# A planner that counts less overlap between instructions, and products of zeros at the start: graph network with attention, one core

## The chip, the core and the metric

The kernel runs on one of the eight cores of a Trainium2 chip. A core has five engines that run beside each other, each with its own queue of instructions in a fixed order: TensorE (PE, matrix products), VectorE (DVE), ScalarE (ACT), GpSimd (POOL) and SyncE (SP, which here only issues DMAs). They wait for each other by semaphores. Products land in PSUM, which has eight banks; everything else works from SBUF. The metric is the device time of one execution in microseconds (us). Unless marked ns, times here are in us.

## What is computed

For each of 128 graphs (128 nodes, 256 features) and an adjacency `adj` of 0 and 1, two layers are applied. Cut to what matters:

```python
def gru_cell(inp, h):                      # w_ih, w_hh: (768, 256)
    gi = inp @ w_ih.T + b_ih
    gh = h @ w_hh.T + b_hh
    r = sigmoid(gi_r + gh_r); z = sigmoid(gi_z + gh_z)
    n = tanh(gi_n + r * gh_n)
    return (1.0 - z) * n + z * h

h = maximum(layernorm(x), 0)               # layer 0
for i in range(3):
    m = einsum('bnd,de->bne', h, weight[i])
    aggr = einsum('bst,bsd->btd', A, m)    # A = (adj != 0)
    h = gru_cell(aggr, h)
x = x + h

h = maximum(layernorm(x), 0)               # layer 1
Wh = h @ W
s = Wh.sum(-1)
e = leaky_relu(s[:, :, None] + s[:, None, :], 0.2)
e = where(adj == 0, -inf, e)
x = x + softmax(e, -1) @ Wh
```

## The kernel before

**Tiling and stages.** The graphs go in 32 groups of four. A group has three stages, one for each step of the recurrence, and then its attention. The first two stages (`gru`) work with features on the partitions: their products are the fp32 matmuls of L708, 128x256. The third (`gru_rows`) works with nodes on the partitions: its products are those of L722, 128x384, called "in rows" here. Stages of different groups follow each other by a fixed list (`turns`): in the steady part, layer 0 of group g, layer 1 of group g-1, layer 2 of group g-2. That makes 96 stages, 32 of them in rows.

**A stage's products.** Each large product is split in blocks so that seven products do the work of eight (sums and differences of the blocks are `hs`, from GpSimd, and `gs`, from VectorE). The seven go into six PSUM banks, x_rz, x_n, q_rz, q_n, y_rz and y_n, in the order written in `products`: x (product 1), q (product 5 or 7), y (product 6), y again (7 or 5), x (2), y (3 or 4), q (4 or 3). The bank y holds a running sum that is read off in between: after product 6 ScalarE copies y_rz to `t2_rz` and y_n to `t2_n`, and only then may the next product be added to y; after that product it copies them to `t3_rz` and `t3_n`, to which VectorE adds q (L764). These copies are all in the helper `put` (L754, or L758 and L760 with a bias). In the profile, whose names leave numbers out, t2_rz and t3_rz both read t_rz. So between "y_n, product 6" and "y_rz, the next product" TensorE depends on one ScalarE copy.

**Other work of TensorE.** Sums over edges in bf16 parts (L634, 24 products for a group and step), the attention's weighted sums (L663) and its rows product (L1099), and transposes (L544). It uses two further banks, `misc`.

**The planner.** Nothing of the order is written out by hand except the order of a stage's products among themselves. `op(engine, ns, fn, reads, writes, ...)` records a piece of work with an estimated duration; `Plan.run` then plays a list scheduler: at each step it finds for each engine the earliest time at which any of its ready pieces can start, takes among the pieces that can start then the one with the lowest rank (a latest start time, worked back from due times), and writes it to that engine's queue. The recurrence's products are a chain in fixed order (`bound`); the other pieces of TensorE go in where the next of the chain can't start yet, or where their rank is lower. A piece ends at `done = t + ns`, and its engine is free for the next at `done - OVER[engine]`: OVER is how far the next instruction overlaps the end of this one, in ns. `wait` and `LAG` give the time from a piece's end to its users. `port` serialises GpSimd with those VectorE pieces that share SBUF access with it (`two=True`).

**The start.** `zeros` is a bf16 tile; two products of it (L326) write 0 to the banks y_rz and y_n, which the first real products overwrite. Then `weights()` loads and transposes the weights. SyncE's first DMAs are: the first message weight (tile e), the two halves of w_ih (tile rz), the second message weight, the first rows of x, adj, w_hh, more rows. `turned` (L363) transposes w_ih half by half through PSUM, VectorE and ScalarE copy the results out (L371), and products (L463) compose them with the transposed message weight (L452) into the weight of the edge terms. w_hh is transposed in the same way, and `block_sums` (L382 to L390) makes the sums of blocks that the stages need.

Of the kernel before, what the change touches and what calls it, by code (L numbers as in the profile page):

```python
# [41 lines left out]
class Plan:  # L42
# [5 lines left out]


    LAG = {"PE": 163, "ACT": 0, "DVE": 0, "POOL": 0, "SP": 3600}  # L50
    OVER = {"PE": 0, "ACT": 103, "DVE": 84, "POOL": 42, "SP": 0}
    FLIP, HANDOFF = 56, 120
    SIGNAL = {"PE": 53, "ACT": 36, "DVE": 36, "POOL": 78, "SP": 28}

    def __init__(self, tags):
# [4 lines left out]
    def buf(self, tag):  # L60
        n, kind = self.tags[tag]
        if kind == "free" or kind == "turn":
            b = Buf(tag, tag, None)
            if kind == "turn":
                self.waiting.setdefault(tag, []).append((self.phase, len(self.waiting.get(tag, ())), b))
            return b
        key = (tag, self.group % SETS if kind == "set" else 0)
        uses = self.last.setdefault(key, [])
        b = Buf(tag, key, uses[-n] if len(uses) >= n else None)
        b.slot = (key[1], len(uses) % n)  # L70
        uses.append(b)
        return b

    def op(self, eng, ns, fn, reads=(), writes=(), room=(), due=None, mark=None,
           turn=None, two=False, lag=None, thin=False):

        i, deps = len(self.nodes), set()  # L80
        for b in room:
            if b.prev is not None:
                deps.update(a[0] for a in b.prev.accesses)
        for is_write, group in ((False, reads), (True, writes)):
            for item in group:
                b, lo, hi = item if isinstance(item, tuple) else (item, 0, 1 << 30)
                for j, w, l, h in b.accesses:
                    if (w or is_write) and l < hi and lo < h:
                        deps.add(j)
                if is_write and b.prev is not None:  # L90
                    deps.update(a[0] for a in b.prev.accesses)
        for is_write, group in ((False, reads), (True, writes)):
            for item in group:
                b, lo, hi = item if isinstance(item, tuple) else (item, 0, 1 << 30)
                b.accesses.append((i, is_write, lo, hi))
        deps.discard(i)
        bufs = {id(x[0] if isinstance(x, tuple) else x): (x[0] if isinstance(x, tuple) else x)
                for x in list(reads) + list(writes) + list(room)}
        free = [b for b in bufs.values() if self.tags[b.tag][1] in ("free", "turn")]
        for b in free:  # L100
            b.users.append(i)
            b.left += 1
        self.nodes.append([eng, ns, fn, deps, free, self.due if due is None else due,
                           two or eng == "POOL", self.LAG[eng] if lag is None else lag, thin])
        if due is not None:
            self.chain.append(i)
        if mark is not None:
            self.marks[mark] = i
        if turn is not None:
            self.turns.append((i, turn))  # L110

    def wait(self, i, u):

        a, b = self.nodes[i], self.nodes[u][0]
        return 0 if a[0] == b == "PE" else a[7] + self.SIGNAL[b]

    def run(self):
# [11 lines left out]
        for tag, w in waiting.items():  # L129
            n = self.tags[tag][0]  # L130
# [40 lines left out]
        order, end = [], 0.0  # L171
        while len(order) < len(nodes):
            best = None
            for e, pool in ready.items():
                if not pool:
                    continue
                starts = []
                for i in pool:
                    if i in bound and i != chain[-1]:
                        continue  # L180
                    t = max(clock[e] + (self.FLIP if thin and e == "PE" and not nodes[i][8] else 0), at[i])
                    for b in nodes[i][4]:
                        if b.slot is None:
                            t = max(t, min(slots[b.tag]))
                            if b.tag in waiting and waiting[b.tag][-1] is not b:
                                t = float("inf")
                    starts.append((max(t, port) if nodes[i][6] else t, t, i))
                first = min((t for t, _, _ in starts), default=float("inf"))
                if first == float("inf"):
                    continue  # L190
                asked, i = min(((r, i) for t, r, i in starts if t <= first), key=lambda x: (rank[x[1]], x[1]))
                if best is None or (first, asked) < best[:2]:
                    best = (first, asked, e, i)
            t, _, e, i = best
            ready[e].remove(i)
            if i in bound:
                chain.pop()
            n = nodes[i]
            done = t + n[1]
            clock[e] = done - self.OVER[e]  # L200
            if n[6]:
                port = done - self.HANDOFF
            if e == "PE":
                thin = n[8]
            end = max(end, done)
            for b in n[4]:
                if b.slot is None:
                    if b.tag in waiting:
                        waiting[b.tag].pop()
                    b.slot = (0, min(range(len(slots[b.tag])), key=lambda k: slots[b.tag][k]))  # L210
                    slots[b.tag][b.slot[1]] = float("inf")
                b.left -= 1
                b.done = max(getattr(b, "done", 0.0), done + n[7] + 36)
                if not b.left:
                    slots[b.tag][b.slot[1]] = b.done
            for u in users[i]:
                missing[u] -= 1
                at[u] = max(at[u], done + self.wait(i, u))
                if not missing[u]:
                    ready[nodes[u][0]].append(u)  # L220
            order.append(i)
# [5 lines left out]
def kernel(  # L227
# [84 lines left out]
    op, buf = plan.op, plan.buf  # L312
# [9 lines left out]

    zeros = const.tile([P, GN], BF16, name="zeros")
    nc.vector.memset(zeros, 0.0)
    for kind in ("y_rz", "y_n"):
        nc.tensor.matmul(phys[kind, 0, 0].rearrange("p q n -> p (q n)"), zeros[:, :P], zeros, start=True,  # L326
                         stop=True, skip_group_check=True)


    W = {t: buf(t) for t in ("s_hh", "s_x0", "s_x1", "s_x2", "bias_i", "bias_h", "bias_s", "bias_n", "seed_x",  # L330
# [3 lines left out]
    def bank(early=True):  # L334
        spare.append(spare.pop(0))
        return buf(spare[-1] if early else "misc")
# [14 lines left out]
    def nat(b):  # L351
        return plain(b)[:, :3 * KD * D].rearrange("p (c e) -> p c e", e=D)

    def turned(src, dst, evict, order=range(6)):


        for a in range(2):
            for k in range(KD):
                ps = bank()

                def turn(k=k, a=a, ps=ps):
                    for c in range(3):
                        nc.tensor.transpose(flat(ps)[:, c * P:(c + 1) * P],  # L363
                                            nat(src)[:, order[3 * a + c], k * P:(k + 1) * P],
                                            ident)
                op("PE", 330, turn, [(src, a, a + 1)], [ps])
                to_sbuf(evict[k % len(evict)], 3 * P, ps, dst[k], 3 * P * a)

    def to_sbuf(eng, cols, ps, dst, at):
        copy = nc.scalar.copy if eng == "ACT" else nc.vector.tensor_copy  # L370
        op(eng, 150 + cols, lambda: copy(plain(dst)[:, at:at + cols], flat(ps)[:, :cols]),  # L371
           [ps], [(dst, at, at + cols)])
# [20 lines left out]
    def weights():  # L393
        plan.due, plan.phase = 10 ** 9, -1
        w_hh_nat, w_ih_nat = buf("rz"), buf("rz")
# [13 lines left out]
        for a in range(2):  # L409
            part = slice(3 * a, 3 * a + 3)  # L410
            op("SP", 384 * KB, lambda part=part: nc.sync.dma_start(
                nat(w_ih_nat)[:, part], w_ih.rearrange("(c p) e -> p c e", p=P)[:, part]),
               [], [(w_ih_nat, a, a + 1)], lag=3300)
        plan.due = 10 ** 9
        load(w_hh_nat, nat, w_hh.rearrange("(c p) e -> p c e", p=P), 768)
        plan.due = -10 ** 8
# [14 lines left out]
        op("DVE", 250, n_bias, [W["bias_h"]], [W["bias_n"]])  # L431

        w_hhT, w_ihT = [buf("u"), buf("u")], [buf("x1"), buf("x1")]
        turned(w_ih_nat, w_ihT, ("DVE", "ACT"))

# [4 lines left out]
        for layer in range(L):  # L442
            if layer == 1:
                turned(w_hh_nat, w_hhT, ("DVE", "ACT"), (4, 5, 0, 1, 2, 3))
                block_sums(w_hhT, W["s_hh"], "POOL", 1000)
# [31 lines left out]
        for t, i, b in ((tmp[0], 0, b_ih), (tmp[1], 0, b_hh), (tmp[2], 0, b_hh), (tmp[2], 1, b_ih)):  # L477
            n = t is tmp[2]
# [55 lines left out]
    def flat(b):  # L534
        return ap(b).rearrange("p q n -> p (q n)")
# [679 lines left out]
```

## Time and profile before

| | us |
|---|---|
| median of 3 runs | 2112.8 |
| lowest and highest of them | 2112.46, 2113.26 |
| the profiled execution | 2112.71 |
| its span, first to last instruction | 2110.9 |

| engine | busy, us | instructions |
|---|---|---|
| TensorE, products | 2084.3 | 10624 |
| VectorE | 1680.2 | 3626 |
| ScalarE | 1594.6 | 2977 |
| GpSimd | 921.5 | 881 |

How to read it: a line of a group or a timeline has the source line, the engine, the operation and the tiles as out<-in; in a timeline the first number is the start from the span's beginning and the second the time from the start of the first to the end of the last of a merged row, and what stands in brackets is idle time of the engine before it and what ended it. Matmuls are pipelined and their ends are modelled: each is shown longer than the time to the next one's start. So the distance between starts tells TensorE's pace, and the sum of busy time does not. An fp32 product written once in the program is shown as two records. A step of 0.216 from start to start is the undisturbed pace of a 128x256 fp32 record, 0.323 that of 128x384.

### The profile page before, as it was taken

The numbers are of one execution on the slowest core, as the hardware profiler recorded it, in microseconds if no ns is written. First come the engines' busy times: TensorE is split into PE (matmuls) and PEld (weight loads), VectorE is DVE, ScalarE is ACT, GpSimd is POOL, SyncE is SP. The second block draws the span as 40 slices with busy tenths as digits, with TensorE's granted clock in tenths as the row PEclk, the third lists the DMA queues.
The fourth block names the chain that finished last, engine by engine and source line by source line (L and its number), as shares of the span: only waits on it lengthen the run. The fifth ranks groups of instructions, "written<-read, shape, count | busy, mean of one in ns | idle before, by whom it ended". The sixth has DMA issues, their size and how long they took to land.

```text
span 2110.9 us, 30632 instructions
## 1 busy us (share of the span) xinstructions
PE 2084.3 (99%) x10624; PEld 1658.4 (79%) x10624; DVE 1680.2 (80%) x3626; ACT 1594.6 (76%) x2977; POOL 921.5 (44%) x881
## 2 busy tenths in 40 slices
PE   9999999999999999999999999999999999999998
PEld 7887887777877778877778777788777888788776
DVE  6678888788877887878878778887787778778777
ACT  5577877777777777777777777777778877867676
POOL 5445554334444444443355434444443444345230
PEclk9999999999999999999999999999999999999999
DMA  4322222332233223232223332232322323123321
GB/s 120 70 59 48 56 57 65 71 60 55 68 68 80 55 54 72 68 73 70 55 61 63 73 74 57 55 75 63 78 60 55 70 64 78 36 55 66 77 74 36
DMA packets 365147, 137.01 MB, mean 65 GB/s; under 512 B 296384, under 2 KB 364736, under 8 KB 364992
## 3 DMA queue, kind: packets, MB, share of 16 engines
q1 hardware_dynamic: 364992, 135.05, 29.1%
q8 instruction: 84, 1.38, 0.3%
q14 instruction: 71, 0.58, 0.1%
HBM read 45.36 MB, written 16.78 MB: 29 GB/s over the span
## 4 chain that ended last, share of the span: by engine, by line
PE 79%; ACT 10%; DVE 7%; issue 2%; DMA 0%; POOL 0%; SPq 0%; DVEq 0%; ACTq 0%; POOLq 0%
PE y_rz L708 14%; PE x_rz L708 10%; PE q_rz L708 8%; PE y_n L708 7%; PE y_rz L722 5%; PE misc L1099 5%; PE y_n L722 5%; PE misc L634 5%; PE x_n L708 4%; PE q_n L708 4%; PE q_rz L722 3%; PE x_n L722 3%; PE x_rz L722 3%; PE q_n L722 3%; ACT h L530 2%
## 5 line engine op out<-in xcount | busy, mean ns | idle before, releaser
L677 POOL TENSOR_TENSOR hs<-hT 128x512 f32<-128x512 f32 x96 | 129.5, 1350 | 304.5 <-PE y_n L722 238.9
L591 POOL TENSOR_TENSOR r<-rows 128x512 f32<-128x512 f32 x126 | 143.0, 1154 | 225.3 <-ACT rows L574 160.9
L764 DVE TENSOR_TENSOR t_rz<-t_rz,q_rz 128x512 f32<-128x512 f32 x192 | 130.8, 681 | 132.5 <-ACT t_rz L754 123.4
L754 ACT COPY t_rz<-y_rz 128x512 f32<-128x512 f32 x192 | 112.2, 584 | 146.4 <-PE y_rz L708 136.1
L708 PE MATMUL y_rz<-hs,s_hh 128*128 128x256 f32 x768 | 200.0, 383 | 1.0 <-ACT t_rz L754 0.9
L708 PE MATMUL y_rz<-gs,s_x 128*128 128x256 f32 x768 | 197.1, 379 | 0.0
L708 PEld LDWEIGHTS y_rz<-hs,s_hh 128*128 128x128 f32 x768 | 142.8, 190 | 27.1 <-ACT t_rz L754 9.2
L708 PEld LDWEIGHTS y_rz<-gs,s_x 128*128 128x128 f32 x768 | 145.9, 190 | 19.8
L594 POOL TENSOR_TENSOR p<-r 128x512 bf16<-128x512 f32 x126 | 156.9, 1264 | 0.0
L681 POOL TENSOR_TENSOR hs<-hT,hs 128x256 f32<-128x256 f32 x96 | 75.3, 785 | 177.1 <-PE q_n L722 160.7
L834 ACT ACTIVATE u<-u,bias_i 128x512 f32<-128x512 f32 x128 | 92.8, 725 | 74.0 <-DVE u L825 73.8
L764 DVE TENSOR_TENSOR t_n<-t_n,q_n 128x512 f32<-128x512 f32 x192 | 130.3, 678 | 19.9 <-ACT t_n L754 17.8
L898 POOL TENSOR_TENSOR x<-x,u 128x512 f32<-128x512 f32 x60 | 77.6, 1294 | 147.9 <-ACT u L878 62.8
L708 PE MATMUL x_rz<-hT,s_hh 128*128 128x256 f32 x512 | 131.4, 379 | 0.0
L708 PE MATMUL x_rz<-aT,s_x 128*128 128x256 f32 x512 | 131.4, 379 | 0.0
L840 DVE SCALAR_TENSOR_TENSOR d<-rz,d 128x512 f32<-128x512 f32 x128 | 117.6, 920 | 0.9
L637 ACT COPY aT<-misc 128x512 f32<-128x512 f32 x190 | 102.8, 581 | 18.1 <-PE misc L634 17.9
L616 POOL TENSOR_TENSOR pl<-d,pl 128x512 bf16<-128x512 f32 x64 | 75.7, 1183 | 89.9 <-ACT pl L614 89.8
L708 PE MATMUL y_n<-gs,s_x 128*128 128x256 f32 x384 | 114.3, 379 | 0.0
L708 PE MATMUL y_n<-hs,s_hh 128*128 128x256 f32 x384 | 114.3, 379 | 0.0
L837 DVE TENSOR_TENSOR d<-hT,u 128x512 f32<-128x512 f32 x128 | 107.3, 839 | 8.5 <-ACT u L834 6.3
L611 POOL TENSOR_TENSOR d<-hT,pl 128x512 f32<-128x512 f32 x64 | 85.6, 1339 | 63.7 <-ACT pl L609 59.0
(286 smaller groups left out, 6297.9 us busy)
## 6 DMA issues: line engine op xcount, KB each, us to landing
rows<-in_x_dram SPq DMA_DIRECT2D x32, 512.0 KB, 4.2
x<-in_x_dram SPq DMA_DIRECT2D x32, 512.0 KB, 3.9
out_dram<-x SPq DMA_DIRECT2D x31, 512.0 KB, 2.9
at<-in_adj_dram SPq DMA_DIRECT2D x32, 256.0 KB, 3.2
plT<-pl SPq DMA_TRANSPOSE x186, 3.3
peT<-pe SPq DMA_TRANSPOSE x60, 3.1
e<-in_L_gnn_weight_dram SPq DMA_DIRECT2D x3, 256.0 KB, 3.7
rz<-in_L_gnn_w_ih_dram SPq DMA_DIRECT2D x2, 384.0 KB, 4.3
```

Of the source, the lines that this page charges most:

```text
L591: op("POOL", 1042, lambda part=part: nc.gpsimd.tensor_tensor(ap(r1)[:, part], ap(rows)[:, part], top(rows)[:, part], OP.subtract), [(rows, ...
L594: op("POOL", 1042, lambda part=part: nc.gpsimd.tensor_tensor(ap(p3)[:, part], ap(r1)[:, part], top(r1)[:, part], OP.subtract), [(r1, n, n ...
L634: nc.tensor.matmul(flat(ps)[:, b * N:(b + 1) * N], part(i, b, k), ap(a)[:, b, :], start=(i == 0), stop=(i == 2))
L637: op("ACT", 590, lambda k=k, ps=ps: nc.scalar.copy(ap(dst)[:, k, :], flat(ps)), [ps], [(dst, 2 * k, 2 * k + 2)])
L677: op(eng, cost, lambda: sub(ap(w)[:, 0:2, :], blocks()[:, 1::2, :], blocks()[:, 0:2, :], OP.subtract), [t], [(w, 0, 2)], two=True)
L708: nc.tensor.matmul(ap(bank)[:, half, :], ap(w)[:, i - 1, gate, :], source(i, t, sums), start=(first and c == 0 and m == 0), stop=False, sk ...
L722: op("PE", 645, lambda c=c, w=w, t=t, sums=sums: nc.tensor.matmul(flat(bank)[:, c * P:(c + 3) * P], source(i, t, sums)[:, m * N:(m + 1) * ...
L754: op("ACT", 590, lambda: nc.scalar.copy(ap(t), ap(y)), [y], [t], mark=mark)
L764: op("DVE", 690, lambda: nc.vector.tensor_tensor(ap(t), ap(t), ap(q), OP.add), [q], [t])
L837: op("DVE", 690, lambda j=j, d=d, cols=cols: nc.vector.tensor_tensor(ap(d), ap(hT)[:, j, :], ap(u)[:, cols], OP.subtract), [(hT, lo, hi), ...
L840: op("DVE", 690, lambda d=d, cols=cols: nc.vector.scalar_tensor_tensor(ap(d), ap(rz)[:, 1, cols], 1.0, ap(d), op0=OP.add, op1=OP.mult), [( ...
L1099: nc.tensor.matmul(ap(ps)[:, b, :], ap(uT)[:, k, (m + b) * N:(m + b + 1) * N], ap(w1)[:, k, :], start=(k == 0), stop=(k == KD - 1))
```

## The change

Three things are changed.

The overlap that the planner subtracts falls from 103 to 50 ns for ScalarE, from 84 to 40 for VectorE, and from 42 to -100 for GpSimd (its next instruction is now planned 100 ns after the end of the one before). The old numbers stay in a table, `TRUE`, that nothing reads. A piece of TensorE that the planner starts before 7200 ns is planned with twice its duration. And the second half of w_ih is planned to land 700 ns later. None of these changes an instruction by itself; they change the times by which `run` orders the queues.

Five products of zeros instead of two stand at the program's beginning, and `turned`, when it transposes w_ih, records three more (into y_n) between the two halves, to be run once the first half has landed.

Lines after L360 or so are 11 further on in the new kernel (L754 is L765, L722 is L733, L708 is L719).

```diff
-    OVER = {"PE": 0, "ACT": 103, "DVE": 84, "POOL": 42, "SP": 0}
-    FLIP, HANDOFF = 56, 120
+    OVER = {"PE": 0, "ACT": 50, "DVE": 40, "POOL": -100, "SP": 0}
+    TRUE = {"PE": 0, "ACT": 103, "DVE": 84, "POOL": 42, "SP": 0}
+    FLIP, HANDOFF, COLD = 56, 120, 7200
...
+    def ns(self, i, t):
+        return self.nodes[i][1] * (2 if self.nodes[i][0] == "PE" and t < self.COLD else 1)
...
-            done = t + n[1]
+            done = t + self.ns(i, t)
             clock[e] = done - self.OVER[e]
...
-    for kind in ("y_rz", "y_n"):
+
+    def nought(kind):
         nc.tensor.matmul(phys[kind, 0, 0].rearrange("p q n -> p (q n)"), zeros[:, :P], zeros, start=True,
                          stop=True, skip_group_check=True)
+
+    for kind in ("y_rz", "y_n", "y_rz", "y_n", "y_rz"):
+        nought(kind)
...
-    def turned(src, dst, evict, order=range(6)):
+    def turned(src, dst, evict, order=range(6), fill=0):
         for a in range(2):
+            if a == 1 and fill:
+                op("PE", 216 * fill, lambda: [nought("y_n") for _ in range(fill)], [(src, 0, 1)], [])
             for k in range(KD):
...
-               [], [(w_ih_nat, a, a + 1)], lag=3300)
+               [], [(w_ih_nat, a, a + 1)], lag=3300 + 700 * a)
...
-        turned(w_ih_nat, w_ihT, ("DVE", "ACT"))
+        turned(w_ih_nat, w_ihT, ("DVE", "ACT"), fill=3)
```

## The prediction

> **What bounds the kernel now.** I read the page first, then who TensorE waits for, then one stage's timelines, then the first 20 us.
>
> ```profile
> PE 2084.3 (99%) x10624; PEld 1658.4 (79%) x10624; DVE 1680.2 (80%) x3626; ACT 1594.6 (76%) x2977; POOL 921.5 (44%) x881
> ...
> engine line waited for: us in total, times, longest us
> PE y_rz L722 <- ACT t_rz L754: 14.1, 19, 1.3
> ```
>
> TensorE has work from end to end; no other engine is over 80%. So time can come only from TensorE's own stops, and most of what is printed is one wait, 19 times: the second edge term's product into y_rz, in the stage that is computed in rows (L722), waits for ScalarE's copy t_rz<-y_rz (L754). One of the 19, TensorE first, then ScalarE:
>
> ```profile
> 581.32 0.81 PE L722 MATMUL y_n<-s_hh,hs 128*128 128x384 f32 x2
> 581.97 0.81 PE L722 MATMUL y_n<-s_x,gs 128*128 128x384 f32 x2
> 583.45 0.91 PE L722 MATMUL y_rz<-s_hh,hs 128*128 128x384 f32 x2 [0.68 <-ACT t_rz L754]
> 584.20 0.81 PE L722 MATMUL y_rz<-s_x,gs 128*128 128x384 f32 x2
> 584.85 1.89 PE L1099 MATMUL misc<-w,uT 128*128 128x256 f32 x8
> ...
> 578.74 0.72 ACT L834 ACTIVATE u<-u,bias_i 128x512 f32<-128x512 f32 x1 [1.40 <-DVE u L825]
> 579.36 0.57 ACT L668 COPY uT<-misc 128x512 f32<-128x512 f32 x1
> 579.83 2.08 ACT L530 ACTIVATE h<-x,nm,rs 128x256 f32<-128x256 f32 x4
> 581.87 1.04 ACT L570 COPY pl<-hT 128x1024 uint16<-128x1024 uint16 x1
> 582.82 0.58 ACT L754 COPY t_rz<-y_rz 128x512 f32<-128x512 f32 x1
> ```
>
> Groups of two such products start 0.65 apart, so the third was due at 582.62. It came at 583.45 (0.83 late) and took 0.75 instead of 0.65 before the next: 0.93 lost, 0.25 more than the printed 0.68. Over the 19: 14.1 + 19 x 0.25 = 18.9; I use 18.5, since some of the added pace is rounding. ScalarE had been busy since 578.74, with an L570 directly ahead of the copy. And the eight L1099 products, which wait for nothing here, stand behind the stop, not in it.
>
> The start:
>
> ```profile
> 3.55 0.66 PE L452 MATMUL misc<-ident,e 128*128 128x128 f32 x2 [1.27 <-DMA e<-in_L_gnn_weight_dram]
> 5.33 0.85 PE L363 MATMUL x_rz<-ident,rz 128*128 128x128 f32 x3
> 7.19 0.87 PE L363 MATMUL misc<-ident,rz 128*128 128x128 f32 x3 [1.01 <-DMA rz<-in_L_gnn_w_ih_dram]
> 11.06 2.53 PE L463 MATMUL misc<-x,uT 128*128 128x512 f32 x4
> 14.29 1.88 PE L463 MATMUL misc<-x,uT 128*128 128x512 f32 x4
> ```
>
> The four L463 products at 11.06 took 2.36 to the next start (13.42); the same four at 14.29 took 1.71 (to 16.00). TensorE ran at half pace until about 12.4, with holes before 3.55 and 7.19.
>
> **What the Trainium skill says.** "TensorE: Matmul & The Clock Gate", Part 1: the array starts at half clock and gets full clock after about 3.4 us of sustained activity, in a free-running window. The trace agrees: after the hole at 7.19, 5.2 us of unbroken work at half pace. That products of zeros count as activity no run here shows. "ScalarE: Activation LUTs", in its section "What ACT_TABLE_LOAD costs", has back-to-back activations overlap by about 93 ns; the trace has 0.10 (592 ns each on average for L530, four in 2.08: (4 x 0.592 - 2.08) / 3). So the overlap counted before (103) is true and the new 50 is pessimistic. "SBUF — State Buffer", section "SBUF: two separate sides": VectorE and GpSimd lock each other out of a shared port; the trace has VectorE's L677 at 1.57 beside GpSimd's L591 and at 0.69 elsewhere. GpSimd's planned 1158 for L611 and L616 is 1339 and 1183 in the page, so counting -100 of overlap there is nearer the truth.
>
> **The change, part by part.** The numbers of overlap alter no instruction, only the order that the planner writes. TensorE's products of the recurrence keep their order; what is moved is the unbound work between them (L634, L663, L1099) and the queues of the other engines. I compared the orders of the two programs, by the old line numbers.
>
> *The 18.5 us.* Each of 96 stages has the place y_rz, y_n, then y_rz again behind the copy. Before, 2 of the 32 rows stages and 28 of the 64 others have unbound products in that place; after, 8 and 40. Before, 23 rows stages have them one step too late, behind the stalled y_rz, as above; after, 1. This is what a planner that takes ScalarE to be later must do: it sees the copy late and puts the products ahead. Where it leaves the place empty, it has found the copy in time by a slower ScalarE than the real one. In the steady part the old order repeats every group and the new one every five, so there are five rows stages. With the vector release of u at the same place (578.74) and 0.62, 0.47, 0.51 and 0.95 for L834, L668, one L530 and L570:
> - u, two L668, copy: 580.3.
> - u, two L668, two L570, copy: 582.2, some 0.2 late, but L1099 products (eight in the trace's count, 8 x 0.216 = 1.73) stand in the place.
> - u, four L530, a second u, copy: at least 582.0, just in time if the second u isn't late.
> - L570, L668, L570, L668, copy, from 577.2 on: 580.0.
> - two u, two L668, L614 (0.51), copy: 581.4 if the first u comes at 578.74.
> The copy must start by 582.0. So four of five are free, and one is covered. I keep 2.0 of the 18.5 for the third kind and the irregular groups: -16.5; bounds -18.5 and -10 (the third and fifth kind still lose 0.93, some 9 stages).
>
> *The small lag.* In stages that aren't in rows an empty place costs 0.08 (the group at 561.25 takes 0.94 instead of 0.86). Twelve more are filled: -0.8 (0.94 rounded down for added late copies).
>
> *TensorE's switches* from bf16 to fp32 go from 99 to 100, each 0.05 (the x_n at 574.32: 0.86 for 0.81): +0.05.
>
> *Five products of zeros instead of two.* At half pace 0.43 each (1.65 minus 1.25 is 0.40): five from 1.25 end at 3.4, and the first weights land at 3.42. They are covered; uncovered, +0.1. They and three more in the hole from 5.97 to 7.19 (1.28 at half pace, 0.65 at full) are there for the clock. If they count, full clock comes between 4.7 and 8.1 by the page's 3.4 us. From 7.19 the four L463 groups then run to about 11 instead of 16; but the new order puts a transpose of w_hh third, and w_hh landed at 12.55. So the gain isn't the 2.6 us that half of 7.19 to 12.4 gives, it is bound by that landing: 12.55, plus 0.33, 0.86, 1.0 and 1.7 of work, plus the transposes and the first products, puts the first q_rz<-hs (before at 26.13) at about 21.8, with four L463 (1.7) still to be done: 2.6 ahead, of which later waits for VectorE and GpSimd take some. I take -2.0; bounds -3.3 and +0.5 (no warmth, and the fill in the way).
>
> *The end.* The order of the last two groups changes in detail, after the last stages ScalarE and VectorE feed TensorE one graph at a time. No row prices it: 0, between -2 and +2.
>
> Sum: -16.5 - 0.8 + 0.05 - 2.0 + 0 = -19.2. The profiled execution is 2112.7, its span 2110.9, so 1.8 lies around it; the median is 2112.8. 2112.8 - 19.2 = 2093.6, taken as 2094.
>
> **The rivals.** A change under 0.2% (4.2 us) can't be told from none here.
> - *The stops move* (15%). Five kinds of groups have fifteen stages, each with a copy that a 1.0 us conversion can hold up. For it: the place leaves 0.08 at most outside the rows stages. Against it: the copies are planned late. At 0.45 in half of the 48 empty places (24 in rows, 24 in other stages) 11 us come back: 2104.
> - *Nothing comes of it* (8%): ScalarE's late start is VectorE's doing (u waited 1.40 for it), and VectorE's new order is as late: the 18.5 stays in other stages, the start gives 1 to 2. 2111.
> - *Slower* (8%): in about 4 of 15 steady stages the copy stands behind one or two tanh of u (L834) with nothing in the place, and u waits for VectorE. Page: 53 such waits, 73.8 us, 1.4 each. If u is that late before the copy, each of some 21 stages loses 1.4 + 0.25 = 1.65, 35 in all, for 19 gained: 2128. It decides the sign from 0.9 us a stage. Against it: the planner counts VectorE pessimistically as well.
> - *The zeros don't warm the clock*: only the start's 2.0 goes, 2096; it lies inside the forecast.
>
> **How the numbers follow.** Forecast 69%, with its own range from 2089 (all stops gone, 3.3 at the start) to 2101; stops moved 15%, nothing 8%, slower 8%. The range up to 2107 takes in the moved stops and leaves out the last two and little below: 2089 to 2107. Faster by over 0.2%, that is under 2108.6: 69 + 15 = 84%; same 7%; slower 9%.
>
> **What would show it.** The wait of y_rz L733 (L722) for the copy falls from 19 times to under 6, and 14.1 us to under 3; no other wait of TensorE in the middle is over 3 us in total. Products at 9 to 12 us take half of what they took, and the transposes of w_hh start at about 12.6. TensorE's busy share rises while its busy sum stays within 5 us. It is wrong if u's tanh stands ahead of the waits of TensorE, or if the start's gain is given back before 30 us.

## The result, and the profile after

| | before | after |
|---|---|---|
| median of 4 runs each, side by side, us | 2113.03 | 2085.54 |
| lowest and highest, us | 2112.46, 2115.22 | 2085.41, 2086.84 |
| span of the profiled execution, us | 2110.9 | 2083.8 |
| ratio of the times, with its 95% interval | | 0.9869 (0.9852 to 0.9886) |

The kernel became 27.5 us faster, 1.3%. The forecast was 18.8 us, with a range from 2089 to 2107; the time lies 3.5 us below the range.

The profile's page of the changed kernel, its engine line and the head of the chain that ended last (share of the span by engine):

```profile
PE 2075.7 (100%) x10630; PEld 1662.7 (80%) x10630; DVE 1661.7 (80%) x3626; ACT 1599.6 (77%) x2977; POOL 934.4 (45%) x881
...
PE 99%; DMA 0%; DVE 0%; SPq 0%; ACT 0%; issue 0%; DVEq 0%; ACTq 0%
```

In the kernel before, the same line reads:

```profile
PE 79%; ACT 10%; DVE 7%; issue 2%; DMA 0%; POOL 0%; SPq 0%; DVEq 0%; ACTq 0%; POOLq 0%
```

Now hardly any time on the chain belongs to anyone but TensorE. The waits of TensorE say the same (waiting line, whom it waited for, total, times, longest):

```profile
PE misc L374 <- DMA rz<-in_L_gnn_w_hh_dram: 1.4, 1, 1.4
PE y_rz L332 <- DVE zeros L329: 1.2, 1, 1.2
PE x_rz L1171 <- DVE eT L1169: 0.6, 1, 0.6
...
PE q_rz L1167 <- ACT s_all L1077: 0.3, 1, 0.3
```

The wait of y_rz for ScalarE's copy, 14.1 us in 19 pieces before, is not in the list. What is left are single waits, and all of the larger ones lie at the start or at the end.

A rows stage of the new kernel, TensorE and then ScalarE (start, time, line, what; in brackets the idle time ahead and what ended it):

```profile
509.37 0.81 PE L733 MATMUL y_n<-s_hh,hs 128*128 128x384 f32 x2
510.02 0.81 PE L733 MATMUL y_n<-s_x,gs 128*128 128x384 f32 x2
510.66 0.81 PE L733 MATMUL y_rz<-s_hh,hs 128*128 128x384 f32 x2
511.31 0.81 PE L733 MATMUL y_rz<-s_x,gs 128*128 128x384 f32 x2
```

```profile
506.99 0.58 ACT L679 COPY uT<-misc 128x512 f32<-128x512 f32 x1 [0.31 <-PE misc L674]
509.63 0.58 ACT L765 COPY t_rz<-y_rz 128x512 f32<-128x512 f32 x1 [2.05 <-PE y_rz L733]
```

The second y_rz starts 0.64 after the second y_n group, the undisturbed pace, with nothing put in between. ScalarE had been idle for 2.05 before the copy and waited for TensorE; in the stage shown of before it was the other way round. So in this stage the copy isn't covered by other work, it is simply on time.

The start, TensorE:

```profile
4.78 0.90 PE L374 MATMUL misc<-ident,rz 128*128 128x128 f32 x3
...
6.11 1.26 PE L332 MATMUL y_n<-zeros 128*128 128x512 bf16 x3
7.21 0.49 PE L374 MATMUL misc<-ident,rz 128*128 128x128 f32 x3
...
9.56 1.88 PE L474 MATMUL misc<-x,uT 128*128 128x512 f32 x4
12.82 0.52 PE L374 MATMUL misc<-ident,rz 128*128 128x128 f32 x3 [1.38 <-DMA rz<-in_L_gnn_w_hh_dram]
...
22.61 1.03 PE L719 MATMUL q_rz<-hs,s_hh 128*128 128x256 f32 x4
```

Three transposes of the same size take 0.90 at 4.78 and 0.49 at 7.21: the clock doubled during the three products of zeros, at about 7.0, and not at 12.4 as before. The four 128x512 products at 9.56 take 1.88, where the first four took 2.53 before. Then TensorE waits 1.38 for w_hh. The first product of the edge term's sum, q_rz<-hs, starts at 22.61; before, it was this one:

```profile
26.13 1.03 PE L708 MATMUL q_rz<-hs,s_hh 128*128 128x256 f32 x4
```

But each of these is one execution, and the start differs from one to the next. The kernel of experiment 3 below whose fill is put ahead by hand has the queues of the kernel before for its first 45 us, and there the full clock comes at 9.9 and q_rz<-hs starts at 24.62. Two more executions with the queues of the changed kernel have the full clock at 7.2 and 7.4, and q_rz<-hs at 21.97 and 22.93.

### A ledger that the busy sums don't give

Since matmuls are shown longer than their pace, I add up distances from start to start instead. The undisturbed pace of one record is 0.112 (128x128, fp32), 0.216 (128x256), 0.323 (128x384), 0.429 (128x512) and 0.056 (128x128, bf16), all read off quiet stretches; products of zeros count 0. By this every kernel of this study has 2063.8 us of work, and the rest of its span is loss. I split the loss in the first 40 us, the middle and the last 60 us:

| loss, us | start | middle | end | all |
|---|---|---|---|---|
| before | 11.4 | 27.7 | 7.9 | 47.1 |
| after | 8.6 | 5.4 | 6.0 | 20.0 |
| gained | 2.8 | 22.4 | 1.9 | 27.1 |

The stops of y_rz in the middle are 19.0 us in rows stages and 4.3 us in the other stages before, and 0 and 1.5 us after. Of the 5.4 us that remain in the middle, 98 switches from bf16 to fp32 at 0.055 us each are as much by themselves. (The paces are rounded to a thousandth, which takes some 2 us off the middle of every kernel alike; so sums are good to that, and differences are better.)

How far the ledger varies by itself can be read from kernels whose queues are the same over a stretch. The start of the kernel before has 11.4 and, in the execution with the same first 45 us, 9.9; that of the changed kernel 8.6, 8.9 and 8.0. The middle of the changed kernel has 5.4 and 6.2. So a difference of 1.5 us at the start is no finding.

### The profile page after: what moved, and what is told of

It reads as the page before. It is cut to its first block, busy times and chain, and to the rows that moved or that the text cites. A ratio compares the mean times of both kernels' runs of the same rounds, so it can differ in the third digit from the quotient of the medians.

```text
span 2083.8 us, 30778 instructions
## 1 busy us (share of the span) xinstructions
PE 2075.7 (100%) x10630; PEld 1662.7 (80%) x10630; DVE 1661.7 (80%) x3626; ACT 1599.6 (77%) x2977; POOL 934.4 (45%) x881
## 3 DMA queue, kind: packets, MB, share of 16 engines
q8 instruction: 84, 1.38, 0.3%
## 4 chain that ended last, share of the span: by engine, by line
PE 99%; DMA 0%; DVE 0%; SPq 0%; ACT 0%; issue 0%; DVEq 0%; ACTq 0%
PE y_rz L719 16%; PE q_rz L719 11%; PE x_rz L719 11%; PE y_n L719 8%; PE misc L645 6%; PE y_n L733 6%; PE y_rz L733 6%; PE x_n L719 5%; PE q_n L719 5%; PE misc L1110 5%; PE q_n L733 4%; PE x_n L733 4%; PE q_rz L733 4%; PE x_rz L733 4%; PE misc L674 3%; PE misc L474 1%
## 5 line engine op out<-in xcount | busy, mean ns | idle before, releaser
L602 POOL TENSOR_TENSOR r<-rows 128x512 f32<-128x512 f32 x126 | 150.9, 1217 | 318.5 <-ACT rows L585 171.6
L765 ACT COPY t_rz<-y_rz 128x512 f32<-128x512 f32 x192 | 112.1, 584 | 125.5 <-PE y_rz L719 78.3
L719 PE MATMUL y_rz<-hs,s_hh 128*128 128x256 f32 x768 | 198.9, 382 | 0.0
L719 PE MATMUL y_rz<-gs,s_x 128*128 128x256 f32 x768 | 197.2, 379 | 0.0
L719 PEld LDWEIGHTS y_rz<-hs,s_hh 128*128 128x128 f32 x768 | 144.1, 190 | 22.9 <-ACT t_rz L765 4.7
L719 PEld LDWEIGHTS y_rz<-gs,s_x 128*128 128x128 f32 x768 | 146.2, 190 | 19.5
L719 PE MATMUL x_rz<-hT,s_hh 128*128 128x256 f32 x512 | 131.4, 379 | 0.0
L719 PE MATMUL x_rz<-aT,s_x 128*128 128x256 f32 x512 | 131.4, 379 | 0.0
L622 POOL TENSOR_TENSOR d<-hT,pl 128x512 f32<-128x512 f32 x64 | 80.3, 1256 | 87.1 <-ACT pl L620 40.7
L719 PE MATMUL y_n<-hs,s_hh 128*128 128x256 f32 x384 | 114.4, 380 | 0.0
L719 PE MATMUL y_n<-gs,s_x 128*128 128x256 f32 x384 | 114.3, 380 | 0.0
L1110 PE MATMUL misc<-w,uT 128*128 128x256 f32 x480 | 112.8, 379 | 0.0
L719 PEld LDWEIGHTS x_rz<-hT,s_hh 128*128 128x128 f32 x512 | 97.4, 190 | 19.2
L688 DVE TENSOR_TENSOR gs<-aT 128x512 f32<-128x512 f32 x96 | 78.6, 819 | 37.6 <-ACT aT L648 37.2
L719 PEld LDWEIGHTS x_rz<-aT,s_x 128*128 128x128 f32 x512 | 97.4, 190 | 13.0
```

The lines of the kernel that those rows point to most:

```text
L602: op("POOL", 1042, lambda part=part: nc.gpsimd.tensor_tensor(ap(r1)[:, part], ap(rows)[:, part], top(rows)[:, part], OP.subtract), [(rows, ...
L622: op("POOL", 1158, lambda k=k, r=r: nc.gpsimd.tensor_tensor(ap(r), ap(hT)[:, k], part(pl, k, 0), OP.subtract), [(hT, 2 * k, 2 * k + 2), (p ...
L688: op(eng, cost, lambda: sub(ap(w)[:, 0:2, :], blocks()[:, 1::2, :], blocks()[:, 0:2, :], OP.subtract), [t], [(w, 0, 2)], two=True)
L719: nc.tensor.matmul(ap(bank)[:, half, :], ap(w)[:, i - 1, gate, :], source(i, t, sums), start=(first and c == 0 and m == 0), stop=False, sk ...
L765: op("ACT", 590, lambda: nc.scalar.copy(ap(t), ap(y)), [y], [t], mark=mark)
L1110: nc.tensor.matmul(ap(ps)[:, b, :], ap(uT)[:, k, (m + b) * N:(m + b + 1) * N], ap(w1)[:, k, :], start=(k == 0), stop=(k == KD - 1))
```

## The experiments

All times are medians, ratios are to the kernel before on the same chip. "Rows" and "other" are the ledger's losses at the second y_rz, "filled" and "behind" are counts from the order of instructions: places ahead of the second y_rz with unbound products in them (rows stages, other stages), and rows stages with such products right behind it.

| kernel | us | ratio | start, middle, end | rows, other | filled | behind |
|---|---|---|---|---|---|---|
| before | 2113.03 | 1 | 11.4, 27.7, 7.9 | 19.0, 4.3 | 2, 28 | 23 |
| after | 2085.54 | 0.9869 | 8.6, 5.4, 6.0 | 0, 1.5 | 8, 40 | 1 |
| all three numbers only | 2086.96 | 0.9880 (0.9867 to 0.9894) | 9.7, 5.5, 6.0 | | 8, 41 | |
| start only | 2113.09 | 1.0004 (0.9996 to 1.0012) | 9.4, 30.4, 7.9 | 20.5, 4.9 | 2, 28 | |
| changed, zeros as before | 2087.62 | 0.9882 (0.9869 to 0.9896) | 10.2, 6.0, 6.0 | | 8, 40 | |
| ScalarE's number only | 2094.19 | 0.9917 (0.9904 to 0.9931) | 11.0, 11.9, 7.3 | 0, 5.8 | 7, 39 | 1 |
| VectorE's number only | 2091.76 | 0.9909 (0.9895 to 0.9922) | 8.2, 10.2, 6.5 | 0, 2.1 | 3, 37 | 3 |
| GpSimd's number only | 2118.03 | 1.0034 (1.0021 to 1.0046) | 10.4, 34.6, 7.9 | 0, 25.5 | 2, 38 | 4 |
| changed, GpSimd's old | 2092.96 | 0.9904 (0.9890 to 0.9917) | 8.6, 11.3, 6.4 | 0, 5.5 | 2, 40 | 10 |
| before, fill put ahead by hand | 2091.97 | 0.9909 (0.9894 to 0.9925) | 9.9, 8.6, 7.9 | 0, 4.3 | 25, 28 | |
| changed, fill put behind by hand | 2098.59 | 0.9933 (0.9920 to 0.9945) | 8.0, 18.6, 6.0 | 0, 13.6 | 0, 0 | |
| still less overlap | 2094.02 | 0.9918 (0.9905 to 0.9932) | 10.2, 8.2, 10.3 | 0, 2.3 | 3, 44 | 6 |
| changed, w_hh planned later | 2085.36 | 0.9869 (0.9854 to 0.9884) | 8.5, 5.6, 6.0 | | | |
| changed, run again | 2086.33 | 0.9873 (0.9859 to 0.9886) | 8.9, 6.2, 6.0 | | | |

The changed kernel measured on another chip gives 0.9873: the gain is the kernel's and not a chip's. All kernels compute the whole result.

### 1. Which part of the change does it

The numbers of overlap alone, in the kernel before:

```diff
-    OVER = {"PE": 0, "ACT": 103, "DVE": 84, "POOL": 42, "SP": 0}
+    OVER = {"PE": 0, "ACT": 50, "DVE": 40, "POOL": -100, "SP": 0}
```

> The kernel before with the three new numbers of overlap alone; no zeros added, no doubled start, no later half. Theory A (the order takes the stops out of the middle, the start is a separate gain): the middle's losses fall from 27.7 us to about 5.5 as in the changed kernel, the first 40 us keep theirs (11.4), the end loses 6 to 8; 22 to 24 us under before, ratio 0.989 to 0.990. Rival B (the gain in the middle hangs on the earlier start, for the planner's doubled start shifts the whole plan): the middle keeps 10 or more of its stops; ratio 0.993 or higher.

The changed kernel with the old numbers, so that only the start is new:

```diff
-    OVER = {"PE": 0, "ACT": 50, "DVE": 40, "POOL": -100, "SP": 0}
+    OVER = {"PE": 0, "ACT": 103, "DVE": 84, "POOL": 42, "SP": 0}
```

> The changed kernel with the old numbers of overlap: zeros, doubled start and later half stay. Its order in the middle repeats every group, as before. Theory A: the 19 stops of the rows stages are all there, the first 40 us lose about 8.5 instead of 11.4; 3 us under before, ratio 0.9985. Rival B: 8 us or more under before.

The numbers alone give 25.7 us of the 27.5, by medians, and the interval of their ratio overlaps that of the whole change. In the traces, the queues of this kernel and of the changed one are the same for every engine from 93 us on, and middle and end lose the same, 5.5 and 6.0 against 5.4 and 6.0. So the numbers make the whole gain in the middle and at the end. The start alone gives nothing that can be measured: the ledger has 2.0 us less at the start and 2.7 us more in the middle. That isn't another order: from 71 us on its queues are those of the kernel before. It stops in the same 19 rows stages, some of them for longer, and why was not found. Its waits of TensorE:

```profile
PE y_rz L733 <- ACT t_rz L765: 15.6, 19, 1.5
PE y_rz L719 <- ACT t_rz L765: 1.4, 2, 1.3
PE q_n L1171 <- DVE eT L1169: 1.4, 1, 1.4
```

The 19 waits are all there, and one of 1.4 at q_n in the last group is there as well. This last one stands in the kernel before too, and is gone after: it is the better part of what the end gained, 1.9 us. So the end's gain comes with the order that the numbers give.

The changed kernel with two products of zeros and none between the halves, all planning kept:

```diff
-    for kind in ("y_rz", "y_n", "y_rz", "y_n", "y_rz"):
+    for kind in ("y_rz", "y_n"):
...
-        turned(w_ih_nat, w_ihT, ("DVE", "ACT"), fill=3)
+        turned(w_ih_nat, w_ihT, ("DVE", "ACT"))
```

> The changed kernel with two zero products as before and none between the halves; all of the planning stays. Theory A with the clock: full clock comes after 9 us instead of at 7.0, the L463-type compositions run at half pace to then, and the wait for w_hh at 12.7 hides most of that; 0 to 1.5 us over the changed kernel, ratio 0.987 to 0.988. If the zeros themselves are what the start gains: 2.5 to 3 us over it, ratio 0.9885.

It lies 1.3 to 2.1 us above the changed kernel's two medians, or 1.9 to 2.7 by the ratios, whose intervals overlap; that is between the two cases of the expectation. The ledger of the start has 10.2 instead of 8.6 and 8.9. So the zeros may be worth 1 to 3 us, and neither the times nor the ledger tell it from nothing.

How the 2.8 us of the start divide between the order and the zeros stays open. The numbers alone have 9.7 there, the start alone 9.4, the changed kernel without the added zeros 10.2. VectorE's number alone, with two products of zeros, has 8.2, less than the changed kernel. All of these lie within 2 us of each other, and executions with the same queues are up to 1.5 us apart.

### 2. Which of the three numbers

One number changed at a time, in the kernel before:

```diff
+    OVER = {"PE": 0, "ACT": 50, "DVE": 84, "POOL": 42, "SP": 0}
```

> The kernel before with ScalarE's overlap alone at 50. If the copies' late place in the plan is the cause (ScalarE's own number), the stops of the rows stages go from 19 to 3 or fewer: its order has 7 rows stages filled and 1 late, against 8 and 1 in the changed kernel; 15 to 22 us under before, ratio 0.990 to 0.993. If GpSimd's or VectorE's number does it, 10 or more stops stay; ratio 0.995 or higher.

```diff
+    OVER = {"PE": 0, "ACT": 103, "DVE": 40, "POOL": 42, "SP": 0}
```

> The kernel before with VectorE's overlap alone at 40. In the stage at 583 us ScalarE was late because VectorE's u was 0.87 late, so slack for VectorE should do as much as slack for ScalarE: its order leaves only 3 late products in rows stages instead of 23. 14 to 20 us under before, ratio 0.9905 to 0.9935. If only ScalarE's own number matters, ratio 0.996 or higher.

```diff
+    OVER = {"PE": 0, "ACT": 103, "DVE": 84, "POOL": -100, "SP": 0}
```

> The kernel before with GpSimd's overlap alone at -100. Theory D (the plan is wrong because GpSimd, planned too short, is found at VectorE's port when VectorE wants it; in the stage at 583 us GpSimd's L616 ran 0.9 us later than planned and VectorE's L679 beside it took 1.27 instead of 0.41): the plan becomes true, stops of the middle fall to 12 us or less, ratio 0.990 to 0.994. Rival E (any slack for ScalarE or VectorE does it, GpSimd's number is no matter): its order still leaves 30 of 32 rows stages empty, 10 or more stops stay, ratio 0.995 or higher.

And the changed kernel with GpSimd's number set back:

```diff
-    OVER = {"PE": 0, "ACT": 50, "DVE": 40, "POOL": -100, "SP": 0}
+    OVER = {"PE": 0, "ACT": 50, "DVE": 40, "POOL": 42, "SP": 0}
```

> The changed kernel with GpSimd's overlap back at 42 and the other two new. GpSimd alone at -100 was slower than before by 7 us, so if its number is only harmful or idle: equal to the changed kernel or up to 3 us faster, ratio 0.985 to 0.987. If it does its part once the other two give slack (the order without it has 10 rows stages with their products behind, against 1): 3 to 10 us over the changed kernel, ratio 0.988 to 0.992.

ScalarE's number alone gains 18.4 us and VectorE's alone 19.4; together with GpSimd's they gain 25.7, so they do largely the same thing and can't be added. Each of them removes all of the loss in rows stages. GpSimd's alone costs 6.9 us (2118.03 against 2111.14), and yet it is worth 6.6 us on top of the other two (2092.96 against 2086.33). The waits of the kernel with GpSimd's number alone show where its loss sits:

```profile
PE y_rz L708 <- ACT t_rz L754: 18.1, 20, 2.3
```

That is the same wait with the line of the other stages. The stops left the rows stages and came back in other stages, most of them in places where unbound products stand ahead of y_rz but end before the copy is there. This is the rival "the stops move" of the prediction, as one of the three numbers brings it about. With all three numbers it didn't happen.

### 3. On time, or covered?

The prediction had two ways for a stop to go: the copy comes in time, or unbound products stand ahead of the y_rz that waits. Two kernels separate these by moving nothing but entries of TensorE's queue. First the kernel before, where a rows product of the attention (L1099) that stands right behind the second y_rz of a rows stage is put ahead of it, in 23 stages; all other queues are as they were:

```diff
+    def ahead(order):
+        nodes, place = plan.nodes, {i: n for n, i in enumerate(order)}
+        pe = [i for i in order if nodes[i][0] == "PE"]
+        for n in range(2, len(pe)):
+            y1, y2, w = pe[n - 2], pe[n - 1], pe[n]
+            if y1 in second and y2 == second[y1] and w in unbound and all(place[j] < place[y1] for j in nodes[w][3]):
+                order.remove(w)
+                order.insert(order.index(y1), w)
+        return order
...
-        for i in plan.run():
+        for i in ahead(plan.run()):
```

> The kernel before with one thing moved: in 23 rows stages the eight L1099 records that stand right behind the stopped y_rz stand ahead of it; every other instruction of every engine stays where it was. Theory A (the stop is uncovered work in the wrong place): the stops are hidden under 1.73 us of products, the wait for the copy falls from 19 to 3 or fewer times, 17 to 18.5 us under before, ratio 0.9915. Rival C (the stop only marks that ScalarE and VectorE are late, and they are late for the next thing too): stops of about the same sum appear at the products that follow; ratio over 0.996.

The same place in time as the stage shown in the prediction, TensorE:

```profile
577.12 0.81 PE L723 MATMUL y_n<-s_x,gs 128*128 128x384 f32 x2
577.77 1.89 PE L1103 MATMUL misc<-w,uT 128*128 128x256 f32 x8
579.50 0.81 PE L723 MATMUL y_rz<-s_hh,hs 128*128 128x384 f32 x2
```

The eight products now fill the time until the copy is there, and the whole 19.0 us of the rows stages are gone: 2091.97, 19.2 us less than before. The other stages keep their 4.3 and the end its 7.9. So for the rows stages covering would have been enough.

Then the changed kernel with the unbound products of all 48 filled places moved behind the first product of the second y_rz:

```diff
+    def behind(order):
...
+        for n, y in enumerate(pe):
+            ahead, k = [], n - 1
+            while y in second and pe[k] not in bound:
+                ahead.insert(0, pe[k])
+                k -= 1
+            if ahead and all(place[u] > place[y] for w in ahead for u in users.get(w, [])):
+                for w in ahead:
+                    order.remove(w)
+                at = order.index(y) + 1
+                order[at:at] = ahead
```

> The changed kernel with one thing moved: in the 48 places (8 in rows, 40 in other stages) where unbound products stand ahead of the second y_rz, they stand behind its first product; every other engine's queue stays. Theory A (the products cover copies that are late): the stops come back, 48 times some 0.3 to 1.0 us, 15 to 45 us over the changed kernel, ratio 0.994 to 1.008. Rival F (by the new order the copies come in time anyway, and the cover is incidental): 0.08 each, 4 us or less over it, ratio 0.987 to 0.989.

It takes 12.3 us more than the changed kernel beside it. Its wait of TensorE:

```profile
PE y_rz L720 <- ACT t_rz L766: 5.0, 12, 0.7
```

One of them, TensorE and then ScalarE:

```profile
788.11 0.59 PE L720 MATMUL y_n<-gs,s_x 128*128 128x256 f32 x2
789.39 1.13 PE L720 MATMUL y_rz<-hs,s_hh 128*128 128x256 f32 x4 [0.69 <-ACT t_rz L766]
790.35 1.46 PE L1113 MATMUL misc<-w,uT 128*128 128x256 f32 x6
```

```profile
787.07 0.62 ACT L892 ACTIVATE u<-u 128x512 f32<-128x512 f32 x1
787.60 1.27 ACT L1080 ACTIVATE e<-e,low 128x128 f32<-128x128 f32 x4
788.77 0.57 ACT L766 COPY t_rz<-y_rz 128x512 f32<-128x512 f32 x1
```

Here the copy is late behind the attention's exponentials (L1080), and the six products that would have covered it stand behind the stop. But all of this is in the stages that aren't in rows (L720): their loss goes from 1.5 to 13.6 us. In the rows stages, where eight places were emptied too, not one stop came back. So both ways are at work, each in its own stages: in rows the new order has the copies on time, and elsewhere it covers late copies. The 12.3 us lie outside of both forecasts for this kernel: the theory that expected 15 to 45 us took covering to do the whole work, and its rival, with 4 us or less, none of it.

### 4. More of the same, and the hole at w_hh

If some pessimism is good, is more of it better?

```diff
-    OVER = {"PE": 0, "ACT": 50, "DVE": 40, "POOL": -100, "SP": 0}
+    OVER = {"PE": 0, "ACT": 0, "DVE": 0, "POOL": -200, "SP": 0}
```

> The changed kernel with still less overlap: 0, 0 and -200. If more slack is always as good, the middle stays at about 5.5 us of losses and the time within 2 us of the changed kernel, ratio 0.987 to 0.988. If slack has a price (the planner believes ScalarE or VectorE to be the bound in some stages and lets TensorE wait in the plan, its fills run out): 5 to 12 us over the changed kernel, ratio 0.990 to 0.993. Its order has 6 products late in rows stages against 1.

No: it is 8 to 10 us slower than the changed kernel, by medians and by ratios, though TensorE hardly stops at y_rz in rows stages (0.3 us in one of them) and more of the other places are filled (44). The ledger puts 4.3 of it at the end, 2.8 in the middle and 1.6 at the start; 1.3 of the 2.8 stand at its bf16-to-fp32 switches. The largest wait of TensorE that the changed kernel doesn't have is one in the last rows stages, at 2048.7:

```profile
PE q_rz L733 <- ACT q_rz L760: 1.5, 1, 1.5
```

Last, a kernel that plans w_hh to land later, by which the composing products for q_n go ahead of w_hh's transposes into the hole of 1.38:

```diff
-        load(w_hh_nat, nat, w_hh.rearrange("(c p) e -> p c e", p=P), 768)
+        load(w_hh_nat, nat, w_hh.rearrange("(c p) e -> p c e", p=P), 768, lag=4300)
```

> The changed kernel with w_hh planned to land 1000 ns later, which puts q_n's four composing products ahead of its first transposes; the middle's order has the same counts. If the wait of 1.4 for w_hh is worth what it shows: the q_n products (0.87) fill it, 0.5 to 0.9 us under the changed kernel in the span, the first 40 us lose some 7.8 instead of 8.6. If the start is then set by VectorE and GpSimd: no difference, and another wait of TensorE before 25 us grows by as much.

The hole is gone, and the time is 2085.36 against 2086.33, with overlapping intervals. The full clock is there from 4.9 us on. That isn't the edit's doing, for up to 12.8 us TensorE's queue is that of the changed kernel, which had it at 7.0 and 7.4. A new wait stands in its place, that of L474 for VectorE's copies out of the transposes (L382), 0.9 us. It can't be told from the changed kernel, and no other run lies below that one.

### What the planner believed

The planner also gives an end to its own plan, a figure of the program and no time of the chip. It says 2079.0 for the kernel before and 2080.3 for the changed one, while the chip took spans of 2110.9 and 2083.8. For ScalarE's or VectorE's number alone it says 2080.5 (2093.9 and 2088.8 on the chip), for GpSimd's alone 2079.3 (2116.7), for still less overlap 2088.9 (2092.5). So the changed plan is 1.3 longer and is met to within 3.5; the plan of before was missed by 32. In the rows stage that the prediction shows, counted from its first q_rz at 575.66, the plan had u's activation (L834) at 2.20, the copy at 6.20 and the second y_rz at 6.94; the trace has 3.08, 7.16 and 7.79. The delay is there when VectorE hands u over, and these lines show where it arises, VectorE and then GpSimd beside it:

```profile
576.37 0.69 DVE L677 TENSOR_TENSOR gs<-aT 128x512 f32<-128x512 f32 x1 [0.34 <-ACT aT L637]
577.09 1.27 DVE L679 TENSOR_TENSOR gs<-gs,aT 128x256 f32<-128x256 f32 x1
578.29 0.41 DVE L825 SCALAR_TENSOR_TENSOR u<-u,t_n 128x256 f32<-128x256 f32 x1
```

```profile
576.93 1.16 POOL L616 TENSOR_TENSOR pl<-d,pl 128x512 bf16<-128x512 f32 x1 [2.39 <-ACT pl L614]
```

L679 takes 1.27 here, with L616 running on GpSimd, and 0.42 alone. This holds throughout the kernel before: the 52 that began while a GpSimd instruction ran took 0.78 or more, the 44 others 0.43 at most. All of L679 in the kernel before and its counterpart L690 after (number, then least, median and longest in ns):

```profile
L679 DVE TENSOR_TENSOR gs<-gs,aT x96: 390/936/1278, 29.4 to 2054.9; 128x256 f32<-128x256 f32 x96
```

```profile
L690 DVE TENSOR_TENSOR gs<-gs,aT x96: 407/424/1381, 24.5 to 2032.5; 128x256 f32<-128x256 f32 x96
```

The median moves more than the number of collisions: 52 of these took over 0.6 us before, 39 after. The Trainium skill's page "SBUF — State Buffer", section "SBUF: two separate sides", says that one engine takes the shared port pair for the whole instruction and the other is blocked; these lines agree and put the price at 0.85 us in this place. Yet the collisions aren't the cause of the stops by themselves: ScalarE's number alone removes every rows stop with 49 of the 96 still slow, and GpSimd's alone leaves 36 and makes a slower kernel. Which moved piece has the copies on time in the rows stages was not separated.

## Where the prediction was right, and where it was too small

The mechanism was right: no work of TensorE changes, the stops of y_rz behind ScalarE's copy go, and the start gains a little. What was wrong is the size, and to the same side in every term that was off. The steps that failed are two terms that were priced at almost nothing: the stages that aren't in rows, at 0.8 us, gave 2.8, and the end, at 0, gave 1.9. The lower end of the range, 2089, already had all 18.5 us of rows stops gone and 3.3 us at the start. So these two terms, 2.0 and 1.9 us more than priced, are what took the time below it; the stops in rows add 0.5.

| term of the sum | predicted | measured |
|---|---|---|
| stops in rows stages | -16.5 | -19.0 |
| the small lag in other stages | -0.8 | -2.8 |
| rest of the middle, switches among it | +0.05 | -0.6 |
| start | -2.0 | -2.8 |
| end | 0 | -1.9 |
| sum | -19.2 | -27.1 |

For the end, one row of TensorE's waits before matters, in the last group:

```profile
PE q_n L1160 <- DVE eT L1158: 1.4, 1, 1.4
```

- *"I keep 2.0 of the 18.5 for the third kind and the irregular groups."* This failed: no rows stage stops at all in the changed kernel. The kind that was reckoned 0.2 late and covered isn't late either, as the kernel with the fill behind shows. The stops themselves were sized well, 18.5 against 19.0.
- *"Twelve more are filled: -0.8"*, at 0.08 for an empty place. This term was the mis-sized one by mechanism. It was priced from one group of the steady part, and the stages that lose more, single stops of the early groups at 182, 242 and 368 us, were left out of the sum. All of these other stages together lost 4.3 before and 1.5 after. The 0.08 itself held, before and after, in the empty places without such a stop, and twelve fewer of them are some 1.0 us; the rest is the single stops, none of which is left in the profile after. With the fill behind these stages lose 13.6: what covers them is worth more than 0.08 a place in the new order.
- *"No row prices it: 0"*, of the end. A row did, the wait of q_n shown above. It goes with the new order and stays in the kernels that keep the old one.
- *The start.* First q_rz<-hs forecast at 21.8, found at 22.61; the transposes of w_hh at 12.6, found at 12.82. The gain reads 2.8 instead of 2.0, but with 9.9 to 11.4 for the old start and 8.0 to 8.9 for the new one it is anything from 1.0 to 3.4, so this term isn't shown to be off. The products of zeros count as activity, as assumed; how much of the gain is theirs is open.
- *The rival "the stops move"* was forecast at 15% with 11 us given back. It happened with GpSimd's number alone, where other stages lose 25.5. With all three it didn't, and even with all 48 places emptied by hand the other stages lose no more than 13.6: the copies are less late there than with GpSimd's number alone.
- *The rival "slower", u's tanh ahead of the waits*: no such wait is in the list.
- *The signs.* The wait fell from 19 times to none, no other wait in the middle is over 3 us, the first products are at full pace by 9 us. One sign missed: TensorE's busy sum was to stay within 5 us and fell by 8.6, since the sum includes the modelled ends and the half-pace products, and is no measure of work.

So the range was too narrow on the good side because the 2.0 that were kept back stood against a gain, and because the other stages and the end had 4.3 and 1.4 us to give in the waits and distances of before.

## What to carry to other kernels

A plan that counts each overlap in full was not the best plan here: where one late copy stops the engine that bounds, a few tens of ns of pessimism for every piece of its feeders can let the chip meet the plan, here for 1.3 us of planned time and 27 of real time; still more of it cost 8 to 10. Why just these numbers do it was not shown: what is shown is that the orders they give have the copies on time or covered. Try such numbers together, for GpSimd's alone was a loss and with the others a gain. And reckon what a kernel loses from distances between starts, with every stage in the sum: the busy sum said 99% while 47 us were lost.

## What the runs showed of the hardware

- Products of zeros count for TensorE's clock. Read off the pace of equal products, full clock starts between 4.9 and 8.7 us in the seven kernels with all eight of them and between 8.6 and 12.4 us in the seven kernels with two. In the one at 4.9, TensorE had run five products of zeros (1.25 to 3.36) and about 1 us of transposes, and nothing else.
- Transposes count as well. With VectorE's number alone, full clock came at 8.57, and TensorE had run only two products of zeros and fp32 transposes until then.
- The Trainium skill's "TensorE: Matmul & The Clock Gate", Part 1, names a free-running window of about 3.4 us and sustained activity, without a share. The 5.2 us of work at half pace in the kernel before are more than one such window and less than two. Taking such a window just ahead of each switch, TensorE was busy in it, by the printed ends, for 0.85 to 1.00; the windows before these were busy for up to 0.83 and brought no switch. (Still less overlap is left out: there the switch falls in a hole, between 6.9 and 8.1.) Where the windows lie is inferred, and with so few cases that is where the boundary lay here, and no more.
- A VectorE operation on two SBUF tiles took 0.43 us at most by itself and 1.15 (median of 52) where a GpSimd instruction was running when it began (L679 of the kernel before).
- A stop of TensorE costs about 0.25 us more than the idle time that is printed (19 of them: 14.1 printed, 19.0 by the ledger). 0.10 of it is that the first record after the stop takes that much longer; the rest is that the ends are modelled.
- A switch from bf16 to fp32 products costs 0.055 us, some 100 times in each of these kernels.
